# Regrouping the second layer norms of a two-layer attention and expert kernel: seven batches beside layer 0's last steps, with their norms on GpSimd

## The chip, the cores and the metric

The kernel runs on one core of a Trainium2 chip. Times are microseconds of device time. The engines are named as in the profile: PE (TensorE matmul), DVE (VectorE), ACT (ScalarE), POOL (GpSimd) and SP (SyncE, which only issues transfers here). [...]The core has an on-chip memory, from which all engines work, and eight accumulation banks, into which PE writes.

## What is computed

The input is 8 batches of 512 tokens with 256 features. Two layers follow each other, each of the form x + attention(norm(x)) + feed-forward(norm(x)):

```python
xn = _layernorm(x, axis=-1)
x = x + _L0_attn_ref(xn, ...) + _L0_ffn_ref(xn, ...)   # 16 heads; 8 experts, one for each token
xn = _layernorm(x, axis=-1)
x = x + _L1_attn_ref(xn, ...) + _L1_ffn_ref(xn, ...)   # two causal attentions with a convolution between; low-rank gelu
return x
```

In layer 0's feed-forward every token goes to the one expert whose centroid it is most like; the expert (norm, 256 to 1024, relu, 1024 to 256) gives ye, and the result is alpha * ye + (1 - alpha) * x with alpha a sigmoid. In layer 1's feed-forward, a product of rank 64 leads up to 1024 features, a gelu follows, and a product of rank 64 leads back to 256. The norm between the layers, the second norm, needs layer 0's whole sum for a token: input, attention and expert. It is this norm, with what leads to it, that the change moves.

## The kernel before

The running sum of each batch stays in an on-chip tile `acc[b]` (128 tokens x 4 chunks x 256). The kernel has three stages.

**Layer 0.** Attention runs as 32 jobs (8 batches x 4 groups of 4 heads). The function `run` (L420) goes through steps t = 0 to 268; a job takes 8 steps for its scores (the matmul at L323, then on DVE the row maximum at L340), and 12 steps later 8 steps for its exps (the matmul at L372, the exponential on ACT at L399); between lie four products with the values (L412). When a job is complete, `l0_done` (L840) transposes and divides its output on DVE (L843 to L847) and POOL adds it to `acc` (L851). Scores are only made in steps 0 to 255; in the last 13 steps exps and value products remain. After the matmuls of each step, `Work.fill` (L103) lets other work in. It first takes work with a due time close by (projections, values, the shift of the maxima, which also issues four transfers on SP's queue, L360), and otherwise draws on a generator, `stream` (L782). Each `yield` of a number charges the generator that much; it may draw while the room of the step, which grows by `MOE_PER_STEP` each step, is above zero. A `yield At(n)` makes the generator wait for step n. So the generator's order is that of program text, and the steps give it its pace.

The generator first makes the first norms and the routing, then the 23 expert blocks of 256 tokens. A block gathers its weights with a POOL-issued transfer (L708) and ends with `output` (L763), whose result goes to a DRAM tile `fs_d` in sorted order (L778). When all 23 are done, `second_norm` (L453) follows for the first four batches (`N_LATE = 4`).

`second_norm` does this for a list of batches. It gathers a batch's rows from `fs_d` with four indirect transfers issued by POOL (L462, into one of two `fg` buffers), one batch ahead. Three steps later DVE adds alpha times the rows to `acc` (L477) and takes mean and variance (`Norms.stats`, L219 and L220). After the last batch `Norms.close` (L222) makes reciprocal deviations: DVE, one square root on ACT (L227), DVE. Then for each batch, one step apart, ACT norms four chunks into a tile `yn` (L236), POOL adds the layer 1 biases to `acc` (L486), and one step later PE transposes the normed tile into features (`to_features`, L241; the copies out of the bank are DVE's for one half, L247, and ACT's for the other, L249). Layer 0's attention tail has a single bank for these transposes.

**Layer 1's feed-forward** (L911 to L978). Eight batches, each in four pairs: `ffn_in` (L912) once a batch, `ffn_hidden` (L923; matmul L927, two gelus on ACT, L933) one pair ahead, `ffn_rank` (L938, matmul L940), and `ffn_out` (L945) at a batch's end: a DVE copy (L947), matmuls (L952), and DVE sums into `acc` (L956). The second norms of batches 4 to 7 run here, as the generator `late`, one piece a pair.

```python
        late = second_norm(range(NB - N_LATE, NB), "d", lambda n: n)
        next(late)
        pTs = {0: ffn_in(0)}
```

**Layer 1's attention** with its convolution follows, from L980, and is not touched.

Of the kernel before, what the change touches and what calls it, by code (L numbers as in the profile page):

```python
# [9 lines left out]
F32 = mybir.dt.float32  # L10
# [3 lines left out]
ALU = mybir.AluOpType  # L14
# [5 lines left out]
P = 128  # L20
NB = 8
S = 512
D = 256
NC = S // P
# [12 lines left out]

STEPS = (8, 6)
LEAD = (12, 12)
N_LATE = 4  # L40
MOE_PER_STEP = 2.05
LAG = 7


# [93 lines left out]
def block_kernel(ctx: ExitStack, tc: tile.TileContext, x, a0_wqk, a0_bqk, a0_wv, a0_bv, cent, experts,  # L138
                 a1_wqk, a1_bqk, a1_wv, a1_bv, conv_w, conv_b, out_w, out_b, u1, v1, f_b1, u2, v2, f_b2, out):
    nc = tc.nc  # L140
# [5 lines left out]
    big = ctx.enter_context(tc.tile_pool(name="big", bufs=NB))  # L146
# [5 lines left out]
    acc = []  # L152
# [49 lines left out]
    class Norms:  # L202
# [27 lines left out]
                nc.vector.tensor_scalar(self.rs1, rs[:, 0, :], 1.0, None, ALU.add)  # L230
            nc.vector.scalar_tensor_tensor(self.nm_t, self.mv[:, :, 0], -1.0, rs[:, 0, :], ALU.mult, ALU.mult)

        def norm(self, i, dst):
            for c in range(NC):
                n = i * NC + c
                nc.scalar.activation(  # L236
                    dst[:, c, :], acc[self.bs[i]][:, c, :], AF.Identity, bias=self.nm_t[:, n : n + 1],
                    scale=self.rs[:, 0, n : n + 1],
                )
# [210 lines left out]
            attend(t)  # L450
        work_of.drain()

    def second_norm(bs, nm, pause):  # L453

        norms = Norms(mid, bs, nm, False)
        fgs = {}

        def gather(b):
            fgs[b] = mid.tile([P, NC, D], F32, tag="fg", name=f"fg{b}", bufs=2)
            for c in range(NC):  # L460
                t = b * NC + c
                nc.gpsimd.indirect_dma_start(  # L462
                    out=fgs[b][:, c, :],
                    out_offset=None,
                    in_=fs_d[:, :],
                    in_offset=IndirectOffsetOnAxis(ap=pos_i[:, t : t + 1], axis=0),
                )

        gather(bs[0])
        for i, b in enumerate(bs):  # L470
            if i + 1 < len(bs):
                gather(bs[i + 1])
            yield pause(3)
            for c in range(NC):
                t = b * NC + c
                a = acc[b][:, c, :]
                nc.vector.scalar_tensor_tensor(a, fgs[b][:, c, :], alpha[:, t : t + 1], a, ALU.mult, ALU.add)  # L477
            norms.stats(i)
        norms.close()
        yns = {}  # L480
        for i in range(len(bs) + 1):
            if i < len(bs):
                b = bs[i]
                yns[b] = work.tile([P, NC, D], F32, tag="o", name=f"yn{b}")
                norms.norm(i, yns[b])
                nc.gpsimd.tensor_tensor(acc[b], acc[b], ob_sb.unsqueeze(1).to_broadcast([P, NC, D]), ALU.add)  # L486
            if i > 0:
                b = bs[i - 1]
                t = big.tile([P, 2, S], F32, tag="xT", name=f"yT{b}")
                for k in range(2):  # L490
                    to_features(yns[b], t, 0, k, f"c{b}")
                xT1.append(t)
            yield pause(1)

    xT = []
    pos_i = const.tile([P, NT], I32, name="pos_i")
# [26 lines left out]
    with ExitStack() as l0:  # L523
# [258 lines left out]
        def stream():  # L782

            norms = [first_norms] + [Norms(pre, bs, nm, True) for bs, nm in (((1, 2, 3), "b"), ((4, 5, 6, 7), "e"))]
            of = {b: (n, i) for n in norms for i, b in enumerate(n.bs)}
            xns = {}

            def stats(b):
                of[b][0].stats(of[b][1])

            def norm(b):
                xns[b] = first_norm(*of[b])

            def features(b):
                first_features(b, xns.pop(b))

            def close(i):
                norms[i].close()

            do = {"s": stats, "c": close, "n": norm, "f": features, "a": affinities}  # L800
            for t, pieces in enumerate(FIRST):
                for p in pieces.split():
                    do[p[0]](int(p[1]))
                if t == 1:
                    for n in range(NBLK):
# [12 lines left out]
            yield At(todo.t + 5)  # L818
            banks_experts()
            nxt.features()  # L820
            yield 0.5
            for n in range(NBLK):
                blk = nxt
                for f2 in range(NFC // 2):
                    blk.hidden(f2)
                    yield 1.75
                    if f2 == 0 and n + 1 < NBLK:
                        nxt = Block(moe, n + 1)
                if n + 1 < NBLK:
                    nxt.features()  # L830
                    yield 0.5
                for j in range(TB // P):
                    blk.output(j)
                    yield 3.5
            banks_alone()
            yield from second_norm(range(NB - N_LATE), "c", lambda n: At(todo.t + n))

        todo = Work()

# [71 lines left out]
    with tc.tile_pool(name="ffn", bufs=1, side="right", reuse_waits="tile") as ffn:  # L911
        def ffn_in(b):  # L912
            ps = bank()
            for k in range(2):
                nc.tensor.matmul(
                    ps, lhsT=u1_sb[:, k, :, :].rearrange("p i r -> p (i r)"), rhs=xT1[b][:, k, :],
                    start=(k == 0), stop=(k == 1),
                )
            pT = ffn.tile([P, S], F32, tag="pT", name=f"pT{b}", bufs=2)
            nc.vector.tensor_copy(pT, ps)  # L920
            return pT

        def ffn_hidden(b, c2, pT):  # L923
            ps = [bank("hidden") for _ in range(2)]
            for i in range(2):
                fc, r = 2 * c2 + i, slice(i * RANK, (i + 1) * RANK)
                nc.tensor.matmul(  # L927
                    ps[i], lhsT=v1_sb[r, fc * P : (fc + 1) * P], rhs=pT[r, :], start=True, stop=True
                )
            hT = ffn.tile([P, 2, S], F32, tag="hT", name=f"gT{b}_{c2}", bufs=3)  # L930
            for i in range(2):
                fc = 2 * c2 + i
                nc.scalar.activation(  # L933
                    hT[:, i, :], ps[i], AF.Gelu_apprx_tanh, bias=fb1_sb[:, fc : fc + 1]
                )
            return hT

        def ffn_rank(pq, c2, hT):  # L938
            for i in range(2):
                nc.tensor.matmul(  # L940
                    pq[i * RANK : (i + 1) * RANK, :], lhsT=u2_sb[:, 2 * c2 + i, :], rhs=hT[:, i, :],
                    start=(c2 == 0), stop=(c2 == NFC // 2 - 1),
                )

        def ffn_out(b, pq):  # L945
            qT = ffn.tile([P, S], F32, tag="qT", name=f"fqT{b}", bufs=2)
            nc.vector.tensor_copy(qT, pq)  # L947
            for h in range(2):
                ps = bank()
                for j in range(2):  # L950
                    c = 2 * h + j
                    nc.tensor.matmul(  # L952
                        ps[:, j * D : (j + 1) * D], lhsT=qT[:, c * P : (c + 1) * P], rhs=v2_sb, start=True, stop=True
                    )
                a = acc[b][:, 2 * h : 2 * h + 2, :].rearrange("p c d -> p (c d)")
                nc.vector.tensor_tensor(a, a, ps, ALU.add)  # L956

        share_banks(hidden=banks[:4], mm=banks[4:7])
        late = second_norm(range(NB - N_LATE, NB), "d", lambda n: n)
        next(late)  # L960
        pTs = {0: ffn_in(0)}
        ahead = [(0, 0, ffn_hidden(0, 0, pTs[0]))]
        pairs = [(b, c2) for b in range(NB) for c2 in range(NFC // 2)]
        pq = None
        out_of = None
        for n, (b, c2) in enumerate(pairs):
            next(late, None)
            if c2 == 1 and b + 1 < NB:
                pTs[b + 1] = ffn_in(b + 1)
            if n + 1 < len(pairs):  # L970
                nb, nc2 = pairs[n + 1]
                ahead.append((nb, nc2, ffn_hidden(nb, nc2, pTs[nb])))
            _, _, hT = ahead.pop(0)
            if c2 == 0:
                pq = banks[7]
            ffn_rank(pq, c2, hT)
            if c2 == NFC // 2 - 1:
                ffn_out(b, pq)  # L978
# [238 lines left out]
```

## Time and profile before

| | us |
|---|---|
| median of 3 runs | 2176.61 (2166.74 to 2185.63) |
| the profiled execution | 2178.01 |
| its span in the profile | 2176.2 |
| PE busy | 2069.3 (95%) |
| DVE busy | 1235.2 (57%) |
| ACT busy | 862.9 (40%) |
| POOL busy | 195.5 (9%) |

All stretches below are in microseconds from the start of that span. Layer 0 runs to 1052, the feed-forward from there to about 1176, layer 1's attention after it. A group of instructions is named by its line, engine and tiles. A PE record's end is modelled, so a busy PE need not be a PE at its peak; each f32 matmul of the program appears as two records. The granted clock is the share of full TensorE speed. In the chain of waits, each piece is followed back to what released it; "issue" is time in which an engine waited for nothing that the profile shows.

### The profile page before, as it was taken

The numbers are of one execution on the slowest core, as the hardware profiler recorded it, in microseconds if no ns is written. First come the engines' busy times: TensorE is split into PE (matmuls) and PEld (weight loads), VectorE is DVE, ScalarE is ACT, GpSimd is POOL, SyncE is SP. The second block draws the span as 40 slices with busy tenths as digits, with TensorE's granted clock in tenths as the row PEclk, the third lists the DMA queues.
The fourth block names the chain that finished last, engine by engine and source line by source line (L and its number), as shares of the span: only waits on it lengthen the run. The fifth ranks groups of instructions, "written<-read, shape, count | busy, mean of one in ns | idle before, by whom it ended". The sixth has DMA issues, their size and how long they took to land.

```text
span 2176.2 us, 35488 instructions
## 1 busy us (share of the span) xinstructions
PE 2069.3 (95%) x13664; PEld 1049.0 (48%) x13664; DVE 1235.2 (57%) x3569; ACT 862.9 (40%) x1674; POOL 195.5 (9%) x222
## 2 busy tenths in 40 slices
PE   7997999999999999997698999999999999999998
PEld 4532555555555555552233455555545545554553
DVE  5465454555555555555423666666766666666661
ACT  2343333333333333334442344444444444444442
POOL 4355000000000000004410000000000000000000
PEclk7599999999999999997899899999999999999997
DMA  5013212221221222201100000000000000000000
GB/s 205 1 42 111 93 61 98 97 100 54 103 94 60 91 73 93 102 11 56 58 1 0 2 2 2 2 2 12 2 12 2 12 2 12 2 12 2 12 2 20
DMA packets 37064, 93.53 MB, mean 43 GB/s; under 512 B 5792, under 2 KB 27936, under 8 KB 33952
## 3 DMA queue, kind: packets, MB, share of 16 engines
q0 software_dynamic: 6384, 59.78, 7.5%
q1 hardware_dynamic: 29792, 30.56, 4.3%
q8 instruction: 107, 1.75, 0.3%
q10 hardware_dynamic: 720, 0.93, 0.1%
q14 instruction: 61, 0.50, 0.1%
HBM read 70.03 MB, written 20.45 MB: 42 GB/s over the span
## 4 chain that ended last, share of the span: by engine, by line
PE 80%; DVE 5%; issue 3%; ACT 1%; another core or an unknown queue 0%; POOL 0%; DMA 0%; DVEq 0%; POOLq 0%; ACTq 0%
PE bank L323 26%; PE bank L412 12%; PE bank L746 8%; PE bank L767 8%; PE bank L272 4%; PE bank L1023 4%; PE bank L390 4%; PE bank L372 3%; PE bank L282 2%; PE bank L1041 2%; PE bank L927 1%; PE bank L1075 1%; PE bank L940 1%; DVE jk L343 1%; PE bank L245 1%
## 5 line engine op out<-in xcount | busy, mean ns | idle before, releaser
L399 ACT ACTIVATE e<-bank 128x512 f32<-128x512 f32 (+1 forms) x1280 | 640.2, 552 | 964.6 <-PE bank L372 483.7
L323 PE MATMUL bank<-k,q 32*128 32x512 f32 (+3 forms) x3072 | 778.9, 538 | 24.4 <-DVE m L340 21.0
L372 PE MATMUL bank<-q,k 32*128 32x512 f32 (+3 forms) x3072 | 701.6, 536 | 15.4 <-DMA q<-mT 13.5
L343 DVE CUSTOM_DVE_ANT_0 jk<-bank,cmask 128x512 bf16<-128x512 f32 (+3 forms) x1024 | 502.6, 491 | 238.0 <-PE bank L323 159.3
L323 PEld LDWEIGHTS bank<-k,q 32*128 32x128 f32 x3072 | 304.3, 187 | 390.4 <-issue 165.2
L340 DVE TENSOR_REDUCE m<-bank 128x1 f32<-128x512 f32 x512 | 329.2, 685 | 163.5 <-PE bank L372 121.0
L412 PE MATMUL bank<-e,v 128*32 128x512 f32 (+3 forms) x3072 | 321.7, 506 | 0.7 <-ACT e L399 0.7
L372 PEld LDWEIGHTS bank<-q,k 32*128 32x128 f32 x3072 | 271.2, 187 | 37.1 <-issue 26.9
L746 PE MATMUL bank<-hsT,w 128*128 128x256 f32 x736 | 180.8, 391 | 0.7 <-ACT e L399 0.7
L767 PE MATMUL bank<-w,hT 128*128 128x256 f32 x736 | 169.0, 383 | 0.0
L746 PEld LDWEIGHTS bank<-hsT,w 128*128 128x128 f32 x736 | 134.5, 191 | 70.4 <-issue 53.3
L767 PEld LDWEIGHTS bank<-w,hT 128*128 128x128 f32 x736 | 136.1, 190 | 35.6 <-issue 19.0
L412 PEld LDWEIGHTS bank<-e,v 128*32 128x32 f32 x3072 | 67.9, 109 | 143.1 <-issue 136.9
L390 PE MATMUL bank<-mask_t,ident_bf 128*128 128x128 bf16 (+1 forms) x768 | 124.3, 244 | 0.0
L390 PEld LDWEIGHTS <-ident_bf 128*128 128x128 bf16 x768 | 43.7, 97 | 158.4 <-issue 143.2
L759 DVE TENSOR_SCALAR hT<-bank,w 128x256 f32<-128x256 f32 x92 | 44.5, 484 | 113.4 <-ACT hT L757 113.4
L1023 PE MATMUL bank<-ctxT,cw_sb 128*128 128x256 f32 x384 | 90.0, 383 | 2.1 <-DVE q L262 1.8
L343 DVE DVE_READ_ACCUMULATOR2_ANT m<- 128x1 f32 x1024 | 84.9, 83 | 0.4
L264 ACT ACTIVATE k<-bank,bqk,rows 128x512 f32<-128x512 f32 x64 | 46.2, 773 | 81.5 <-PE bank L272 71.5
L851 POOL TENSOR_TENSOR acc<-acc,og 128x256 f32<-128x256 f32 x32 | 23.2, 726 | 615.2 <-DVE og L847 615.2
L776 DVE TENSOR_TENSOR f<-bank,w 128x256 f32<-128x256 f32 x46 | 19.5, 425 | 101.4 <-PE bank L767 101.4
L1023 PEld LDWEIGHTS bank<-ctxT,cw_sb 128*128 128x128 f32 x384 | 70.1, 189 | 13.2 <-DVE q L262 3.2
(180 smaller groups left out, 1472.4 us busy)
## 6 DMA issues: line engine op xcount, KB each, us to landing
q<-mT SPq DMA_DIRECT2D x384, 2.0 KB
hs_d<-zeros SPq DMA_DIRECT2D x23, 256.0 KB
hs<-hs_d SPq DMA_DIRECT2D x23, 256.0 KB
fs_d<-f SPq DMA_DIRECT2D x23, 256.0 KB
acc<-in_x SPq DMA_DIRECT2D x8, 512.0 KB
out<-acc SPq DMA_DIRECT2D x8, 512.0 KB
cw_sb<-in_conv_w SPq DMA_DIRECT2D x1, 768.0 KB
wqk<-in_a_wqk ACTq DMA_DIRECT2D x1, 512.0 KB
```

What stands on the lines that cost most here:

```text
L264: nc.scalar.activation(dst, ps, AF.Identity, bias=bias[:, half : half + 1], scale=rows[:, half : half + 1])
L272: nc.tensor.matmul(ps, lhsT=w[:, k, col : col + P], rhs=src[:, k, :], start=(k == 0), stop=(k == 1))
L323: lambda h=h, qc=qc, at=at, nk=nk: nc.tensor.matmul(heads[h % 2][:, at : at + nk], lhsT=self.q[h * PH : (h + 1) * PH, qc * P : (qc + 1) * ...
L340: nc.vector.tensor_reduce(self.m[:, qc, h, :], src, AX.X, ALU.max, negate=True)
L343: nc.vector.tensor_tensor_reduce(out=junk[:, :nk], in0=src, in1=cmask[:, S - nk :], scale=1.0, scalar=-3e38, op0=ALU.add, op1=ALU.max, acc ...
L372: lambda h=h, kc=kc, at=at, lo=lo: nc.tensor.matmul(heads[h % 2][:, at : at + S - lo], lhsT=self.k[h * PH : (h + 1) * PH, kc * P : (kc + 1 ...
L390: nc.tensor.matmul(heads[h][:, : len(blocks) * P], lhsT=ident_bf, rhs=mask_t[:, : len(blocks) * P], start=False, stop=True,)
L399: nc.scalar.activation(e[:, h, :], heads[h][:, :n], AF.Exp, scale=self.scale)
L412: nc.tensor.matmul(self.av[h * PH : (h + 1) * PH, lo:], lhsT=self.v[:, kc, 4 * self.g + h, :], rhs=es[h // 2][:, h % 2, :], start=first, s ...
L746: nc.tensor.matmul(ps[:, i * TB : (i + 1) * TB], lhsT=w[:, O_W1 + k * FF + fc * P : O_W1 + k * FF + (fc + 1) * P], rhs=self.hsT[:, k, :], ...
L767: nc.tensor.matmul(ps[:, 0:D], lhsT=self.hT[:, fc, j * P : (j + 1) * P], rhs=w[:, O_W2 + fc * D : O_W2 + (fc + 1) * D], start=(fc == 0), s ...
L1023: nc.tensor.matmul(ps[:, :w], lhsT=cw_sb[:, k, tap, c * P : (c + 1) * P], rhs=ctxT[b % 2][:, k, tap + lo : tap + lo + w], start=(k == 0 an ...
```

## The change

The second norms are no longer two lists of four batches but three groups, of which the first two, with seven batches, run as part of layer 0's generator. The third, batch 7 alone, has its gather and its expert sum there, and the rest in the feed-forward's first pairs. Between the gather of one batch and its sum lie two steps in place of three. The four norms of a batch are POOL `tensor_scalar` instructions (multiply, then add, with two scalars for each partition) in place of ACT's. The experts' allowance a step goes from 2.05 to 2.1.

```diff
-N_LATE = 4
-MOE_PER_STEP = 2.05
+SECOND = ((0, 1, 2, 3), (4, 5, 6), (7,))
+MOE_PER_STEP = 2.1
...
-        def norm(self, i, dst):
+        def norm(self, i, dst, eng=None):
             for c in range(NC):
                 n = i * NC + c
+                if eng is not None:
+                    eng.tensor_scalar(
+                        dst[:, c, :], acc[self.bs[i]][:, c, :], self.rs[:, 0, n : n + 1], self.nm_t[:, n : n + 1],
+                        ALU.mult, ALU.add,
+                    )
+                    continue
...
+    def second_norm(norms, i):
+
+        b = norms.bs[i]
+        yn = work.tile([P, NC, D], F32, tag="o", name=f"yn{b}")
+        norms.norm(i, yn, nc.gpsimd)
+        nc.gpsimd.tensor_tensor(acc[b], acc[b], ob_sb.unsqueeze(1).to_broadcast([P, NC, D]), ALU.add)
+        return yn
...
+    def second_norms():
+
+        gather(0)
+        for g, bs in enumerate(SECOND):
+            norms = Norms(mid, bs, "cde"[g], False)
+            seconds_of.append(norms)
+            for i, b in enumerate(bs):
+                if b + 1 < NB:
+                    gather(b + 1)
+                yield At(todo.t + 2)
+                add_experts(b)
+                if g < 2:
+                    norms.stats(i)
+            if g == 2:
+                return
+            yield At(todo.t + 1)
+            norms.close()
+            yns = {}
+            for i in range(len(bs) + 1):
+                if i < len(bs):
+                    yns[i] = second_norm(norms, i)
+                if i > 0:
+                    second_features(bs[i - 1], yns.pop(i - 1))
+                yield At(todo.t + 1)
...
             banks_alone()
-            yield from second_norm(range(NB - N_LATE), "c", lambda n: At(todo.t + n))
+            yield from second_norms()
...
-        late = second_norm(range(NB - N_LATE, NB), "d", lambda n: n)
-        next(late)
+        def late():
+            norms = seconds_of[-1]
+            yield
+            norms.stats(0)
+            yield
+            norms.close()
+            yield
+            yn = second_norm(norms, 0)
+            yield
+            second_features(norms.bs[0], yn)
+
+        rest = late()
...
-            next(late, None)
+            next(rest, None)
```

The functions `gather`, `add_experts` and `second_features` hold what stood inside `second_norm` before: the four gathers of a batch, its four DVE sums, and its transposes.

More of the change, by code (lines that the diff above doesn't have):

```diff
@@ L451, in run @@
         work_of.drain()
[L453 to L493, printed above, removed]
@@ new lines, in block_kernel, with gather, add_experts @@
+    fgs = {}
+    seconds_of = []
+    def gather(b):
+        fgs[b] = mid.tile([P, NC, D], F32, tag="fg", name=f"fg{b}", bufs=2)
+        for c in range(NC):
+            t = b * NC + c
+            nc.gpsimd.indirect_dma_start(
+                out=fgs[b][:, c, :],
+                out_offset=None,
+                in_=fs_d[:, :],
+                in_offset=IndirectOffsetOnAxis(ap=pos_i[:, t : t + 1], axis=0),
+            )
+    def add_experts(b):
+        for c in range(NC):
+            t = b * NC + c
+            a = acc[b][:, c, :]
+            nc.vector.scalar_tensor_tensor(a, fgs[b][:, c, :], alpha[:, t : t + 1], a, ALU.mult, ALU.add)
@@ new lines, in second_norm, with second_features @@
+    def second_norm(norms, i):
[4 more added lines that the diff above has]
+        return yn
+    def second_features(b, yn):
+        t = big.tile([P, 2, S], F32, tag="xT", name=f"yT{b}")
+        for k in range(2):
+            to_features(yn, t, 0, k, f"c{b}")
+        xT1.append(t)
+    def second_norms():
[21 more added lines that the diff above has]
+                yield At(todo.t + 1)
```

## The prediction

> **What bounds the kernel now.** I read the 40 slices first, then a table of stretches cut at the stage borders, then the chain of waits and the order of time inside the bad stretches. The slices (54.4 us each) show TensorE full except at the start and around slices 18 to 21:
>
> ```profile
> PE   7997999999999999997698999999999999999998
> ```
>
> The table of stretches (columns: stretch, its length, busy us of PE, weight loads, DVE, ACT, POOL with instruction counts, granted clock, DMA share, GB/s):
>
> ```profile
> 900.00:966.00 66.00, 64.81 (x364) 33.80 (x357) 35.05 (x64) 24.76 (x46) 2.41 (x3) 1.00 0.13 47
> 976.00:1008.00 32.00, 23.61 (x109) 6.75 (x105) 20.17 (x47) 9.46 (x18) 16.21 (x17) 0.76 0.26 75
> 1008.00:1052.00 44.00, 34.60 (x153) 11.09 (x145) 13.38 (x37) 28.21 (x51) 10.13 (x5) 0.82 0.09 27
> 1052.00:1081.00 29.00, 15.70 (x48) 4.33 (x45) 18.85 (x57) 7.46 (x13) 16.28 (x17) 0.77 0.33 101
> 1112.00:1173.00 61.00, 57.07 (x209) 19.56 (x210) 13.01 (x19) 24.00 (x39) 0.00 (x0) 1.00 0.00 0
> ```
>
> Up to 976 (the last expert matmul ends at 975.6) PE is the bound at full clock. 976 to 1052 is layer 0's tail: attention steps 246 to 268 without expert work, with the first four second norms. 1052 to 1173 is the feed-forward stage; its first 29 us hold the other four. In the three stretches from 976 to 1081 PE has gaps and a clock near 0.8. The reader is to see that the change can win only between 976 and 1100, about 6% of the span.
>
> In the feed-forward stage the PE-bound rhythm is read from the chain of waits: the copies of a batch's rank-64 result start at
>
> ```profile
> 1098.91 0.70 DVE fqT L947
> ...
> 1111.91 0.70 DVE fqT L947
> ...
> 1124.91 0.70 DVE fqT L947
> ```
>
> 13.0 us per batch. The first such copy starts only at 1080.15, 28.1 us after the stage's first matmul (1052.0), and the second 18.8 us later. In the order of time, ACT sits from 1066.0 to 1079.5 at the square root of the late norms, behind four batches of gathers, sums and statistics on DVE; the gelus behind it wait, and PE waits for them.
>
> In the tail, this chain piece stands out, with PE, DVE and ACT all standing:
>
> ```profile
> 989.54 6.97 another core or an unknown queue
> ```
>
> It ends just after the gather traffic does (last packets before 996). No view names its cause.
>
> **What the Trainium skill says.** TensorE: Matmul & The Clock Gate, What's actually happening: PE's clock halves after an idle window and comes back after a busy one. The trace agrees: clock 0.50 from 990 to 998, where an AV group takes 1.94 us instead of 1.06. So a PE gap costs more than its length. ScalarE: Activation LUTs, What ACT_TABLE_LOAD costs: some 1283 ns for each change of set; the trace has 1.28 us at each of the loads at 1017.0, 1022.6, 1064.8, 1082.4. GPSIMD Engine Reference, Engine selection: one-input elementwise work is roughly line-rate there, two-input work about twice slower than on VectorE. The trace agrees for one form and not for another, which is my main unknown:
>
> ```profile
> L565 POOL TENSOR_SCALAR acc<-acc,rs1e,nme x16: 552/553/555, 161.3 to 207.3; 128x256 f32<-128x256 f32 x16
> ...
> L553 POOL TENSOR_SCALAR h<-acc,mve,rse x16: 1222/1228/1237, 55.7 to 73.8; 128x256 f32<-128x256 f32 x16
> ...
> L486 POOL TENSOR_TENSOR acc<-acc,ob_sb x8: 2348/2354/2368, 1022.7 to 1095.0; 128x1024 f32<-128x1024 f32 x8
> ...
> L236 ACT ACTIVATE yn<-acc,nmc,rsc x16: 584/594/608, 1020.5 to 1036.8; 128x256 f32<-128x256 f32 x16
> ```
>
> (from the answers by line and by tile: count, then min/median/max ns). The new norm on POOL multiplies and adds with two per-partition scalars, as L565 does (553 ns), but writes another tile, as L553 does (1228 ns, subtract then multiply). I take 0.553, as the operation pair is the same; 1.23 is the upper end, and below 0.553 nothing in the trace gives a reason to go.
>
> **The change part by part.** Following the planner's rule (room per step, costs, due times), before: last expert output in step 245, gathers from 246, sums in 249, 252, 255, 258, norms 258 to 261. After: last expert output in step 240, end seen in 242, sums of batches 0 to 3 in 244, 246, 248, 250, close and norms 251 to 254, features to 255, gather 5 in 256, sums 4 to 6 in 258, 260, 262, close and norms 263 to 265, features to 266; batch 7's sum falls in the final drain, after step 268.
>
> *More expert work per step.* Nothing in sum while PE is full: 64.81 of 66 us busy. Attention of steps 241 to 245 moves behind the experts: 5 x 1.29 (scores and exps matmuls) + 2 x 1.05 (AV) + 0.2 = 8.8 us, so experts end at 966.8. The expert weight loads on POOL's queue come 2.4% closer together, hidden: POOL is busy 5 us in 100 there. Bounds from other stalls: PE idles about 8 us between 300 and 900, so some 3 us either way.
>
> *Steps 241 to 243*: 2.07 us each, as steps 246 to 250 take now: 973.0.
>
> *Steps 244 to 250*: DVE is the bound. Per batch four sums at 0.41 spacing (1.65) and four statistics pairs at 0.53 and the rest (2.3), 3.95 us; per step two max reductions, 1.29; one output transpose group 1.4; one shift copy 0.3. So 4 x 3.95 + 7 x 1.29 + 1.7 = 26.5; plus 1 us because the first sum, two steps rather than three after its gather, meets rows that land about 9.5 us after the last expert result (979.13, the first gather now, is 3.5 after it; four at 1.25; landing 1): 1000.5. DVE's sums stand ahead of the reductions that free score banks, so PE waits behind them.
>
> *Steps 251 to 255*: reductions 1.3 and close 1.2, to 1003. Then POOL in order: norm 4 x 0.553 = 2.21, bias add 2.35, and PE's transposes (in program order between attention steps) wait for each norm. Four norms with three bias adds between: 8.8 + 7.1 = 15.9, to 1019. ACT did this norm in 2.07 beside POOL's add; now both are serial, 4.6 per batch. Last features 2, and 3 for cold-clock matmuls (transposes 1.12 instead of 0.66 per four): 1024. Removed: 16 ACT norms, 8.3 us, that stood between the exps.
>
> *Steps 256 to 262*: 7 x 1.93 (1041 to 1051 has 3.85 for two such steps), to 1037.5; sums, statistics, gathers 5 to 7 (5 us each on POOL) run beside it. The third of these gathers ends near 1040, and close near 1041.
>
> *Steps 263 to 268*: three norms, two adds: 6.6 + 4.7 = 11.3, features 2, two steps 3.9: 1058.5. Now 1052.0, so the tail ends **6.5 us later**. The extra table pair of the second close (2.6 us) lies on an ACT that only has two exps a step, 1.09; no queue waits for more than that, so I give it the same cover as the waits above.
>
> *SP's queue* gets no new transfer in the tail; a shift transfer of 4 parts in step 249 and one in 257 now meet more gather traffic, with three steps until the exps need them: nothing, or 3 us if they land late.
>
> *Feed-forward stage.* First rank matmul 4.7 us after the start (1056.7 - 1052.0), 7 batches at 13.0, last batch's four pairs 10.3: 106.0. Added: batch 7's sum ahead of the first copy on DVE 1.65, its 8 transposes 1.1, two table loads 2.6 of which ACT's slack (gelus take 1.27 of each 3.05 us pair) hides about 1.1, 1.5 left. 110.3 against 121.2 (1052.0 to 1173.2). The stall goes; the next late thing is PE itself. **10.9 us won**; with a last copy counted from 1174.4 it is 12.3; I use 12. If batch 7's close blocks the gelus as the late norms do now, 5 of it go.
>
> Sum: +6.5 - 12 = -5.5. The profiled execution took 2178.0 (span 2176.2, 1.8 around it), 1.4 above the median 2176.6. So 2172.5 on its scale, **2171** on the median's.
>
> **Rivals.** *Room in the tail* (faster). The 7 us stall is an accident that does not come back, and POOL's norms overlap better than the sum allows, ACT being free. Then the tail is what PE needs: 1045 now without the stall, less ACT's queue at 1020 to 1040 (5), plus three batches of features (6.6), less the idle before the close (4): 1042.6, so -9.4 - 12 = -21: 2155. For it: ACT is busy 14.87 of the 20 us from 1020. Against: DVE's 26.5 us is arithmetic on the same instructions.
>
> *POOL as the bound* (slower). Norms at L553's 1.23: 28 x 0.675 = 19 more on the norm chain: tail at 1077, +25 - 12 = +13: 2190; with a repeat of the 7 us stall under 28 gathers, 2197. It decides from about 0.75 us a norm (5.5 / 28 above 0.553). For it: L553, and DVE's sums with two SBUF inputs run beside it. Against: L565's operations.
>
> *It does not do what it says*: norms slip past step 268 into the drain. The planner's dates exclude it for all but batch 7; 2 in 100, at about the time of before.
>
> **From cases to numbers.** Forecast 58, room 25, POOL 15, nothing done 2. For 1% (21.8 us, about what a measurement of this kernel can tell from no change): below 2155 lies half of the room case and a little of the forecast's spread, 0.19; above 2198 a third of POOL's, 0.05; the rest 0.76. The range takes the forecast's unknowns (3 expert phase, 5 cold clock, 3 shift, 5 close; about 12 together), most of the room case and half of POOL's: 2151 to 2190.
>
> **What would show it.** Last expert matmul near 967; norms on POOL at 0.55; first feed-forward matmul near 1058; first rank copy under 22 us after it; 13.0 between the rest. Wrong if the feed-forward start comes before 1046 or after 1068, or POOL's norm is over 0.75.

## The result and the profile after

| | before | after |
|---|---|---|
| median, same chip | 2176.07 (8 runs) | 2194.68 (8 runs; 2191.65 to 2205.81) |
| ratio | | 1.0093 (95% interval 1.0068 to 1.0118) |
| the profiled execution | 2178.01 | 2192.13 |
| its span | 2176.2 | 2190.4 |

The change makes the kernel 0.9% slower: 14.2 us between the two profiled spans, where 5.5 were to be won. All stretches below are microseconds from the start of the span of the kernel named.

The 40 slices of the kernel after, its rows for PE and for the granted clock (tenths):

```profile
PE   7997999999999999997898999999999999999998
...
PEclk7599999999999999998799799999999999999997
```

By the slices PE is as full as before. What differs must be looked for in the stretches. The table of stretches of the kernel after (stretch, length, busy us of PE, weight loads, DVE, ACT, POOL, granted clock, DMA share, GB/s):

```profile
900.00:966.00 66.00, 64.82 (x350) 34.67 (x349) 34.30 (x62) 23.68 (x44) 2.41 (x3) 0.97 0.13 47
976.00:1012.00 36.00, 28.24 (x143) 7.75 (x141) 29.78 (x74) 13.08 (x23) 20.18 (x21) 0.86 0.28 81
1012.00:1052.00 40.00, 29.20 (x147) 9.77 (x147) 24.59 (x63) 18.71 (x34) 31.02 (x34) 0.91 0.20 63
1052.00:1074.00 22.00, 17.54 (x57) 6.50 (x60) 2.36 (x5) 7.68 (x13) 13.48 (x15) 0.55 0.01 5
...
1112.00:1173.00 61.00, 56.91 (x206) 18.65 (x205) 12.40 (x18) 24.08 (x39) 0.00 (x0) 1.00 0.00 1
```

976 to 1074 is the tail. From 976 to 1012 DVE is the busiest engine (29.78 of 36 us: sums, statistics, row maxima); from 1012 to 1052 POOL is (31.02 of 40 us: norms, bias additions, gathers); from 1052 on PE is (17.54 of 22 us), at a clock of 0.55.

The chain of waits of the kernel after shows the feed-forward's rank copies:

```profile
1093.02 0.70 DVE fqT L971
...
1106.90 0.70 DVE fqT L971
...
1119.90 0.70 DVE fqT L971
```

The first starts 18.4 us after the stage's first matmul (1074.6), where 28.1 were needed before; the second 13.9 us after it, not 18.8; then 13.0 each, as before. This part of the change works. The tile view of the norms on POOL (count, min/median/max ns):

```profile
L237 POOL TENSOR_SCALAR yn<-acc,rsc,nmc x16: 549/556/559, 1014.2 to 1030.6; 128x256 f32<-128x256 f32 x16
L237 POOL TENSOR_SCALAR yn<-acc,rsd,nmd x12: 544/552/556, 1052.5 to 1063.2; 128x256 f32<-128x256 f32 x12
```

So the time is lost ahead of that stage and behind it. Four marks divide the span: the last expert matmul's end, the feed-forward's first matmul, the start of its last rank copy, and the first division of layer 1's attention (L1044 in the kernel before).

| stretch | before | after | difference | predicted |
|---|---|---|---|---|
| experts, to their last matmul | 975.7 | 976.5 | +0.8 | -8.8 |
| tail, to the first feed-forward matmul | 76.3 | 98.1 | +21.8 | +15.3 |
| feed-forward, to its last rank copy | 122.4 | 107.8 | -14.6 | -12 |
| layer 1's lead-in, to its first division | 60.7 | 67.3 | +6.6 | 0 |
| the rest of layer 1 | 941.1 | 940.7 | -0.4 | 0 |

The predicted +15.3 of the tail is 6.5 + 8.8: the prediction counted the tail's end, and its start was to come 8.8 earlier. Two terms failed outright, the experts and the lead-in; the tail was over 40% dearer. Both columns are single executions: the tail before, 76.3 us here, was 67.3 and 81.2 us in two other profiles of the same instructions, so the tail's difference lies between 17 and 31 us.

### The profile page after: what moved, and what is told of

The parts are those of the page before. It is cut to its first block, busy times and chain, and to the rows that moved or that the text cites. A ratio compares the mean times of both kernels' runs of the same rounds, so it can differ in the third digit from the quotient of the medians.

```text
span 2190.4 us, 35505 instructions
## 1 busy us (share of the span) xinstructions
PE 2080.9 (95%) x13664; PEld 1053.3 (48%) x13664; DVE 1236.7 (56%) x3572; ACT 850.5 (39%) x1645; POOL 212.5 (10%) x254
## 4 chain that ended last, share of the span: by engine, by line
PE 82%; DVE 5%; issue 2%; ACT 1%; POOL 0%; DMA 0%; SPq 0%; DVEq 0%; ACTq 0%; POOLq 0%
PE bank L329 26%; PE bank L418 12%; PE bank L770 8%; PE bank L791 8%; PE bank L278 5%; PE bank L396 4%; PE bank L1057 4%; PE bank L378 3%; PE bank L288 2%; PE bank L1075 2%; PE bank L951 2%; PE bank L964 1%; PE bank L1109 1%; PE bank L251 1%; DVE m L346 1%
## 5 line engine op out<-in xcount | busy, mean ns | idle before, releaser
L405 ACT ACTIVATE e<-bank 128x512 f32<-128x512 f32 (+1 forms) x1280 | 640.1, 552 | 978.8 <-PE bank L378 507.8
L378 PE MATMUL bank<-q,k 32*128 32x512 f32 (+3 forms) x3072 | 705.6, 539 | 15.7 <-DMA q<-mT 13.8
L800 DVE TENSOR_TENSOR f<-bank,w 128x256 f32<-128x256 f32 x46 | 19.5, 424 | 108.9 <-PE bank L791 108.9
```

The source lines that it names most:

```text
L378: lambda h=h, kc=kc, at=at, lo=lo: nc.tensor.matmul(heads[h % 2][:, at : at + S - lo], lhsT=self.k[h * PH : (h + 1) * PH, kc * P : (kc + 1 ...
L405: nc.scalar.activation(e[:, h, :], heads[h][:, :n], AF.Exp, scale=self.scale)
```

## The experiments

All ratios are to the kernel before on the same chip. The letters in the expectations: theory A, that the higher allowance brings no earlier end of the experts; rival C, that the serial chain of norms and bias additions on POOL sets the tail; theory D came after the first four runs and is told with the ones that follow. PE's busy time in one fixed stretch of the expert phase, 230 to 966, carried most of it. The other columns are the stretches above, in us ("rest" is the rest of layer 1):

| kernel | PE busy, 230 to 966 | last expert matmul | tail | feed-forward | lead-in | rest | ratio |
|---|---|---|---|---|---|---|---|
| before | 726.1 | 975.7 | 76.3 | 122.4 | 60.7 | 941.1 | |
| before_leadin | 726.1 | 973.6 | 67.3 | 122.1 | 59.6 | 943.7 | 1.0016 |
| paced_late | 726.1 | 976.6 | 81.2 | 118.8 | 61.0 | 941.1 | 0.9996 |
| gathers_apart | 726.2 | 977.1 | 85.2 | 124.8 | 65.5 | 933.3 | 1.0002 |
| allow21_alone | 720.8 | 974.2 | 95.3 | 122.1 | 64.7 | 945.8 | 1.0146 |
| allow206 | 720.4 | 982.5 | 94.6 | 123.1 | 60.6 | 946.7 | 1.0087 |
| odd_filled | 733.5 | 964.4 | 74.0 | 124.0 | 63.8 | 941.1 | 0.9952 |
| odd_leadin | 733.5 | 967.7 | 75.1 | 122.5 | 59.6 | 945.4 | 0.9971 |
| after | 720.8 | 976.5 | 98.1 | 107.8 | 67.3 | 940.7 | 1.0093 |
| warm_leadin | 720.8 | 978.8 | 98.1 | 107.8 | 59.4 | 943.2 | 1.0042 |
| warm_tail | 720.8 | 976.4 | 98.1 | 107.8 | 67.3 | 940.7 | 1.0100 |
| norms_on_act | 720.7 | 976.1 | 118.0 | 106.8 | 65.6 | 946.7 | 1.0117 |
| bias_last | 720.7 | 978.6 | 109.7 | 106.8 | 60.7 | 941.0 | 1.0088 |
| regroup_205 | 726.2 | 977.0 | 102.4 | 108.3 | 64.7 | 933.5 | 1.0030 |
| change_odd_filled | 732.7 | 954.5 | 111.0 | 106.8 | 67.2 | 946.6 | 0.9992 |
| change_odd_leadin | 733.0 | 952.0 | 100.7 | 107.7 | 59.4 | 943.3 | 0.9982 |
| change_odd_warm | 734.1 | 955.7 | 117.5 | 107.9 | 59.4 | 944.9 | 0.9975 |

The ratios are over many executions; the stretches are of one each, and they differ between executions of the same instructions. Up to the feed-forward, before, before_leadin and paced_late are the same program, with tails of 76.3, 67.3 and 81.2 us; so are change_odd_filled and change_odd_leadin, with 111.0 and 100.7. The end of the experts differs by up to 3.7 us in this way, and the rest of layer 1, the same instructions in all, takes 933.3 to 946.7 us. A smaller difference than these between two rows says nothing by itself. PE's busy time in the expert phase agrees within 1.4 us.

### The allowance alone

```diff
-MOE_PER_STEP = 2.05
+MOE_PER_STEP = 2.1     # in the kernel before
```

> The kernel before with the experts' allowance at 2.1 and nothing else. Theory A (the higher allowance itself loses what the earlier end should have won): last expert matmul at 974 to 978 although it now belongs to step 240, so the five attention steps behind it come on top; feed-forward starts near 1061 instead of 1052, time 2184 to 2188. Rival B (the allowance costs nothing, all of the loss lies in the regrouped norms): last expert matmul near 967, feed-forward start 1050 to 1054, time within 4 us of before.

Measured: 1.0146 (1.0115 to 1.0176). The last expert matmul ends at 974.2, 1.5 us earlier instead of 8.8, which is within the spread of the kernel before, and the tail behind it grows to 95.3 us. The part of the change that was to shorten the expert phase makes the kernel slower by itself. In the profile most of that lies in the tail, 19.0 us longer where five attention steps make 8.8.

### Norms on ACT again, and bias additions behind the norms

```diff
-        norms.norm(i, yn, nc.gpsimd)     # norms_on_act, in the kernel after
+        norms.norm(i, yn)
```

> The changed kernel with its second norms back on ACT, all else kept. Theory A (the norms' engine is not the cause, PE comes late anyway because of the clock and of DVE): feed-forward starts within 4 us of 1074.6, time 2190 to 2199. Rival C (the POOL chain of norm and bias add, 4.6 us a batch, sets the pace): ACT's 2.1 us a batch lets the feed-forward start 8 us or more earlier, time 2187 or less.

Measured: 1.0117 (1.0086 to 1.0148); the feed-forward starts at 1094.1, 19.5 us later than with the change. Neither expectation came. Two pieces of 6.4 and 7.8 us without a named cause stand in this tail (more on such pieces below), and the interval overlaps that of the change (1.0068 to 1.0118), so this shows no gain from ACT's norms, but not that POOL's are better.

```diff
-        nc.gpsimd.tensor_tensor(acc[b], acc[b], ob_sb...)   # bias_last: out of second_norm,
+            for b in bs:                                    # and behind all norms of a group
+                add_biases(b)
```

> The changed kernel with POOL's bias adds after the last norm of each group instead of between the norms. Theory A: PE waits mostly for DVE and for its own clock, so the feed-forward starts at most 4 us earlier than 1074.6, time 2190 to 2195. Rival C (serial POOL chain): five bias adds of 2.35 us leave the chain, feed-forward starts about 11 us earlier, time 2183.

Measured: 1.0088 (1.0056 to 1.0121), the change's own ratio within its interval, with the feed-forward starting at 1088.3, later. Two pieces without a named cause make 10.0 of the 13.7 us, and the experts end 2.1 later. Rival C is not borne out: its 2183 us would be a ratio of 1.003, below the interval. In this run the stretch from 1060 to 1088 has a clock of 0.55.

### The late norms paced, nothing moved into the tail

The kernel before, where batches 4 to 7 stay in the feed-forward but in two groups (4, 5) and (6, 7), with gathers, sums, norms (on POOL) and transposes spread over 15 pairs by hand.

```diff
-        late = second_norm(range(NB - N_LATE, NB), "d", lambda n: n)
-        next(late)
+        LATE = ("g4", "", "g5", "s4", "g6", "s5", "cd", "n4 g7", "n5 f4 s6", "f5", "s7", "ce", "n6", "n7 f6", "f7")
+        late = paced()     # g gathers, s sums, c closes, n norms, f makes features
```

> The kernel before with its four late batches kept in the feed-forward stage but spread over 15 pairs in two groups of two: a gather every second pair, the sum three pairs after its gather, square root and norm a pair apart, norms on POOL. If the stall of the stage was only one of order (waits queued ahead of the gelus and of the rank copies), the tail stays as before (start at 1052), the first rank copy comes 17 to 20 us after the start, the last near 1162, time 2162 to 2167. If transfers or table loads hold the stage up anyway, time 2174 or more.

Measured: 0.9996 (0.9972 to 1.002). The first copy comes 19.1 us after the stage's start, but the next ones at 16.0, 19.4 and 14.8 us, not 13.0: the one stall of 28 us became several small ones (6.4 of the 19.1 us are again a piece without a named cause). The expected gain did not come; the ratio answers to the rival's 2174 us or more.

### Why a higher allowance loses PE time

The order of time on PE in the kernel after, near the end of the experts (start, us, line, tiles; in brackets the idle time before and what ended it; lines 329 and 378 are the matmuls of scores and exps, 418 the value products, 791 an expert's):

```profile
968.26 1.06 PE L418 MATMUL bank<-e,v 128*32 128x512 f32 x8
969.25 0.70 PE L329 MATMUL bank<-k,q 32*128 32x512 f32 x2
969.27 0.70 PE L378 MATMUL bank<-q,k 32*128 32x512 f32 x2
969.79 0.59 PE L329 MATMUL bank<-k,q 32*128 32x512 f32 x2
969.80 0.59 PE L378 MATMUL bank<-q,k 32*128 32x512 f32 x2
971.16 1.29 PE L329 MATMUL bank<-k,q 32*128 32x512 f32 x3 [0.76 <-DVE m L346]
```

The step that starts at 969.25 got no expert work: its scores are followed at once by those of the next step, at 971.16, and these wait 0.76 us for DVE's row maxima to free a bank. While experts run only two banks hold scores (`banks_experts`), one step's worth. A step that has a value product or expert work covers the maxima; value products come only in even steps. This is theory D: in an **empty odd step** PE waits up to 1.2 us (9.9 us in 12 waits in the kernel before, 0.8 on average), and it is the allowance's size against the pieces' charges that decides how many such steps there are. The planner's rule gives 11 at 2.05, 21 at 2.06 and 19 at 2.1, up to the experts' end. The waits of PE from 230 to 966 (us in total, times, longest), before:

```profile
PE bank L323 <- DVE m L340: 9.9, 12, 1.2
```

and after:

```profile
PE bank L329 <- DVE m L346: 15.2, 18, 1.2
```

The 5.3 us more are the 5.3 us that PE's busy time falls in that stretch. This reading agrees with the Trainium skill, Perfetto Trace Analysis, Optimization Strategy: the same gap repeating on the engine that should be saturated can mean too few buffers for the next tile. No run gave the scores a third bank, which would test that directly; the runs below change only how many steps go empty.

An allowance hardly above the old one, and two kernels with a rule that lets no odd step go empty (a charge is taken in advance if need be), test it:

```diff
-            if not forced and (n == most or self.room <= 0):
+            if not forced and (n == most or (self.room <= 0 and (n > 0 or t % 2 == 0))):
                 return
...
                     self.room -= cost
+                    n += 1
```

> The kernel before with the allowance at 2.06 in place of 2.05. By the planner's rule the last expert output moves by one step only (244 for 245), but the steps that hold neither expert or projection work nor a value product rise from 11 to 21. Theory D (in such a step PE waits about 1 us for the row maxima, as only two banks hold scores): last expert matmul at 983 to 986, PE's waits for the maxima between 230 and 966 rise from 9.9 to 15 us or more, time 8 to 14 us above before. Rival E (what costs is the pace itself, or the longer tail after the experts): 0.01 of allowance changes nothing, last expert matmul at 974 to 976, time within 3 us of before.

> The kernel before at 2.05 with one rule more in the planner: in a step without a value product (odd steps) one piece of work is drawn even when the allowance is used up. Last expert output stays in step 245; steps with nothing in them fall from 11 to 5. Theory D: last expert matmul 5 to 7 us earlier, at 969 to 971, time 2170 to 2172 on the first chip's scale, 5 to 7 us below before. Rival E: within 2 us of before.

> The changed kernel with the same rule: last expert output in step 239 instead of 240, steps with nothing in them fall from 19 to 4. Theory D: last expert matmul at 960 to 963 instead of 976.5, feed-forward start at 1058 to 1063 instead of 1074.6, time about 14 us below the changed kernel, so within 6 us of before. Rival E: as the changed kernel, 0.9% above before.

Measured: with 2.06 the ratio is 1.0087 (1.0057 to 1.0117), the waits 15.6 us in 22 times, the last expert matmul at 982.5: half a per cent of allowance costs 0.9% of time. With the rule in the kernel before the ratio is 0.9952 (0.9927 to 0.9977), the last expert matmul at 964.4 and the waits

```profile
PE bank L324 <- DVE m L341: 2.3, 4, 0.6
```

With the rule in the changed kernel: 0.9992 (0.9977 to 1.0007), the last expert matmul at 954.5, 22 us earlier than with the change, and the waits at 1.7 us in 3 times. So theory D holds for the expert phase: in each of the three runs PE's waits and the end of the experts move as it says. With the rule the experts end 11.3 and 22.0 us earlier, of which 7.6 and 13.5 are waits for row maxima that are gone; the rule also draws work ahead of its allowance, and the rest was not told apart.

The theory does not cover the tail. Of what allow206 loses in its profile, 6.8 us lie in the expert phase and 18.3 in the tail, whose mean clock is 0.66 where the kernel before has 0.80; why is not known. With the rule in the changed kernel 13 of the 22 us go to a tail of 111.0 us, but 4.5 of these are a piece without a named cause, and change_odd_leadin, the same program up to there, has 100.7.

### The 7 us stall

In the kernel before a stall of 6.97 us at 989.5 had no named cause. It ended with the gathers' traffic; if gathers that overlap cause it, gathers held back take it away. The edit, shown without the flag that keeps it to the tail's four batches:

```diff
-            if i + 1 < len(bs):
-                gather(bs[i + 1])
             yield pause(3)
...
                 nc.vector.scalar_tensor_tensor(a, fgs[b][:, c, :], alpha[:, t : t + 1], a, ALU.mult, ALU.add)
+            if i + 1 < len(bs):
+                gather(bs[i + 1])
             norms.stats(i)
```

> The kernel before with the tail's gathers issued one batch at a time, each after the sum of the batch ahead of it, so that no two batches of row transfers follow each other without a gap. Theory F (the 7 us in which PE, DVE and ACT stand is set off by eight row gathers in a row): no such piece in the chain of waits between 976 and 1050, tail 69 to 73 us instead of 76 to 81, time 4 to 8 us below before. Rival G (it comes from something else, or the later gathers only move the wait to DVE's sums): a piece of 4 us or more is still there, or the sums wait that long, time within 3 us of before or above.

Measured: 1.0002 (0.9986 to 1.0018). No such piece is in this tail's chain of waits, but the tail is 85.2 us, with a clock of 0.50 from 1030 to 1060. Inconclusive. Such pieces of 2 to 8 us are in the tails of 8 of the 17 profiles here, before among them, and not in that of the kernel after. They do not go with the program: before_leadin has none and ends its tail after 67.3 us, with the same instructions up to there. All four profiles from one chip have them, none of the seven from two others. Their cause stays open.

### The regrouping alone, and the cold clock

```diff
-MOE_PER_STEP = 2.1      # regroup_205, in the kernel after
+MOE_PER_STEP = 2.05
...
+            if layer == 0 and t >= 259:     # warm_tail; in warm_leadin: layer == 1 and t < lead, banks[6]
+                nc.tensor.matmul(banks[0], lhsT=ident, rhs=xT1[0][:, 0, :], start=True, stop=True)
             work_of.fill(t, per_step, most)
```

The added matmul writes a bank that is free there, and nobody reads it.

> The change with the allowance back at 2.05: regrouping and POOL norms alone. Theory D (the higher allowance makes steps in which PE waits for row maxima, and gives no earlier end) expects the last expert result at 975.7 as before (976.5 with the change), and puts a price of about 15 us on the higher allowance in the kernel before; but here it also moved the second group's norms in front of step 268, and at 2.05 the norms of batches 5 and 6 fall behind step 268 with nothing beside them. So a tail of 100 to 110 us (98.1 with the change), the feed-forward at 107 to 108, time 2185 to 2200. The rival, that the allowance is the whole loss and the regrouping is worth its -5.5 us: tail under 90, time 2165 to 2175.

> The change with one more f32 matmul, 128x128 by 512 columns, in each of steps 259 to 268 of layer 0, whose result nobody reads: ten times about 0.9 us of PE work at full clock, mostly where PE waits now (8.9 us idle between 1050 and 1080). If the halved clock is what makes the tail's last part long (from 1052.5 to 1074.6, 22.1 us, clock 0.50 to 0.57), the clock stays over 0.8 there and the stretch from the fourth norm's start to the feed-forward takes 17 to 20 us, time 3 to 6 us under the change's. If the chain of norms on POOL sets it and the clock is only its companion, the stretch stays at 22 or grows to 30 and the time is the change's or up to 9 us more.

> The change with one more such matmul in each of the first 12 steps of layer 1, into a bank that is free then. From the last rank copy to the first token division the change takes 67.3 us with the clock at 0.50 to 0.75 between 1200 and 1240, before 60.7. Twelve matmuls are 10 us of PE work at full clock. If the light steps let the clock fall (PE waits for row maxima there), the clock is near 1.00 and the lead-in takes 58 to 64 us in spite of the added work: time 2185 to 2192. If the clock falls for another reason, the lead-in is 75 to 80 us and the time 2202 to 2208.

> The change with the rule for odd steps and both sets of added matmuls. With that rule alone the tail was 111 us (954.5 to 1065.5), the lead-in 67.2, time 2183. If the cold clock is the reason that the 22 us won in the expert phase were given back, the tail is 98 to 103, the lead-in 58 to 64, time 2165 to 2172, under the kernel before and about the best so far (2174.6). If not, 2190 to 2203.

Measured for **regroup_205**: 1.0030 (1.0009 to 1.0051), tail 102.4. PE's busy time in the expert phase is back at 726.2 and the waits at 9.9 us. So at 2.05 the regrouping loses 0.3%, and the allowance 0.6% on top (1.0093 against 1.0030). In the other order the allowance loses 1.5%, and the regrouping then wins 0.5% (1.0093 against 1.0146). The two parts do not simply add up: by the planner's rule, at 2.05 the norms of batches 5 and 6 fall behind step 268, with nothing beside them. Neither pair was run on one chip.

For **warm_tail**: 1.0100 (1.0066 to 1.0134), no gain. The clock from 1052 to 1074 rose from 0.55 to

```profile
1052.00:1074.00 22.00, 18.16 (x76) 6.51 (x74) 2.47 (x5) 10.98 (x17) 13.51 (x15) 0.92 0.06 15
```

and the stretch from norm 4's start (1055.0) to the feed-forward's start (1074.5) took 19.4 us, in place of 22.1. But the four added matmuls in it are 4.2 us of PE work, and those ahead of it made norm 4 start 2.5 us later. By this count, an estimate (19.4 less 4.2), the halved clock lengthens the tail's last part from some 15 us to 22; extra work does not buy it back.

For **warm_leadin**: 1.0042 (1.0023 to 1.0062), half a per cent under the change. The lead-in of the kernel after, from 17.7 to 63.7 us behind the last rank copy:

```profile
1200.00:1246.00 46.00, 43.97 (x193) 20.36 (x192) 24.86 (x94) 10.01 (x19) 0.00 (x0) 0.67 0.00 1
```

and with the added matmuls:

```profile
1202.00:1248.00 46.00, 45.70 (x267) 19.74 (x265) 30.14 (x111) 13.82 (x26) 0.00 (x0) 1.00 0.01 1
```

PE is busy in both, but after the change a record lasts longer: the clock is 0.67, and 193 matmul records fit where 267 do with the clock at 1.00 (24 of them the added ones). Twelve more matmuls, an estimated 12 us of work by their 1.05 us in warm_tail, make the lead-in 8 us shorter.

For **change_odd_warm**, with the rule for odd steps and both sets: 0.9975 (0.9952 to 0.9997), a median of 2172.2 us. The lead-in is 59.4 us as expected; the tail is 117.5 us, not 98 to 103, so that half of the expectation missed, as warm_tail did. The profiled execution, at 2187.1 us, is the second slowest of 21, and says little of where the median's gain lies.

### Does the cold lead-in belong to the change?

The added matmuls of warm_leadin in three other kernels: the kernel before, odd_filled and change_odd_filled.

> The kernel before with the twelve added matmuls in layer 1's first steps. If the cold lead-in belongs to the change, the lead-in here goes from 60.7 to 60 or more (its clock is lifted only from 0.66 to 0.86 up, and 10 us of work are added): ratio 0.999 to 1.003. If it is a habit of every arrangement, in the mean over runs the clock in the lead-in is as low here as there, and the time falls by 0.3 to 0.5% (the changed kernel went from 1.0093 to 1.0042): ratio 0.995 to 0.997.

> The kernel before with the rule for odd steps and the added matmuls. Alone the rule gave 0.9952. If the two add up: 0.990 to 0.993, 2159 to 2165 us beside 2180. If the lead-in gains nothing in this arrangement: 0.995 to 0.998.

> The change with the rule for odd steps and the added matmuls in layer 1 only. With the rule alone 0.9992, with both sets of added matmuls 0.9975. If the regrouping by itself is worth its -5.5 us when expert phase and lead-in are equal, this is 0.2 to 0.3% under odd_leadin: 0.988 to 0.990. If its longer tail takes back what the feed-forward wins, it is 0.2 to 0.5% above odd_leadin: 0.994 to 0.997.

Measured: before_leadin 1.0016 (1.0000 to 1.0033), nothing gained: its lead-in is 59.6 us, before it was 60.7. odd_leadin 0.9971 (0.9954 to 0.9988), change_odd_leadin 0.9982 (0.9968 to 0.9996). By the rule set down for before_leadin, the cold lead-in would belong to the change. The profiles do not bear that out. With the added matmuls the lead-in is 59.4 to 59.6 us in every kernel. Without them it is 67.2 to 67.3 us in after, warm_tail and change_odd_filled, but 60.7 in bias_last, which has the change too; and gathers_apart, which has not, takes 65.5 us with a clock of 0.67. Nor is the gain of 0.5% found again: with the rule for odd steps, the added matmuls move the changed kernel from 0.9992 to 0.9982, with intervals that overlap. In the stretch of the kernel before that answers to the one shown, the clock is

```profile
1192.00:1238.00 46.00, 44.26 (x225) 19.91 (x222) 29.53 (x110) 12.89 (x24) 0.00 (x0) 0.81 0.01 1
```

The instructions there are the same in both kernels. So a low clock makes the lead-in long, which warm_leadin shows; what lets it fall in one kernel and not in another stays open.

With the rule and the warm lead-in in both, the change is worth nothing that can be told: 0.9982 against 0.9971, with intervals that overlap, medians of 2167.2 and 2169.6. In the profiles its experts end 15.7 us earlier and its feed-forward is 14.8 us shorter, and 25.6 of these 30.5 us go into a tail of 100.7 us in place of 75.1. The lowest ratio is that of odd_filled, the kernel before with one rule changed, at 0.9952; odd_leadin, which adds the matmuls, is no better.

## Why the prediction was wrong, point by point

**The step that failed** is the first of the sum, "More expert work per step. Nothing in sum while PE is full". It moved 8.8 us of attention behind the experts and let them end at 966.8. They ended at 976.5. The count of 64.81 busy us in 66 was right for the kernel before, but it is no property of PE: it was what that allowance left. PE waits, 0.8 us on average, in the empty odd steps, and the new allowance made eight more of them. 5.3 us of the 9.7 missing are seen as lost busy time from 230 to 966, 0.8 at 971; the other 3.6 have no account, where the prediction left 3 open either way. That the empty steps are the cause is shown by the rule that fills them: with it the changed kernel's experts end at 954.5, and its ratio falls from 1.0093 to 0.9992. In the ratios the allowance costs 0.6% with the regrouping and 1.5% without it, where the step counted nothing in sum. The other two terms, +6.5 and -12, make -5.5 us, or -0.25%, for the regrouping; it measured +0.3% at 2.05, where its norms fall behind step 268, and -0.5% at 2.1.

**Layer 1's lead-in** had no term: +6.6 in the profile, and warm_leadin shows that the clock makes it. Since bias_last, with the change, has none of it, a term for the change would not have been right either. The prediction's range had 5 us for the cold clock in the tail only.

**The tail's steps**, measured from the experts' end, follow the prediction until the last: sums and statistics end at +35.5 (+33.7 predicted), the four norms with features at +58.0 (+57.2), steps 256 to 262 take 13.6 (13.5), norm 4 starts at +76.0. Then 22.1 us where "11.3, features 2, two steps 3.9" make 17.2. The term was mis-sized by the clock. The order of time on PE after shows it:

```profile
1053.10 2.08 PE L251 MATMUL bank<-ident,yn 128*128 128x128 f32 x4 [2.09 <-POOL yn L237]
1055.96 1.11 PE L251 MATMUL bank<-ident,yn 128*128 128x128 f32 x4 [0.79 <-DVE yT L253]
1057.01 1.94 PE L418 MATMUL bank<-e,v 128*32 128x512 f32 x8
1058.88 2.08 PE L378 MATMUL bank<-q,k 32*128 32x512 f32 x4
```

Each group takes nearly twice its time at full clock (1.11 for 0.66, 1.94 for 1.06). PE waited for the first norm of the second group, and behind that wait the clock is low; with the clock at 0.92 in warm_tail, the same part took 19.4 us with 4.2 us of added matmuls in it. The prediction's own remark that a PE gap costs more than its length was applied to 3 us of transposes, and not to the attention steps behind them.

**Right**: in the tail DVE is the busiest engine during the sums and POOL during the norms; a POOL norm takes 0.55 us, so the rival of POOL as the bound is wrong, although its 2190 lies close to what came; the 7 us stall did not return, which is luck, since such pieces come and go between executions of one program; SP's queue cost 0.2 us at most where PE waits for a shift (1041.7); the feed-forward won 14.6 where 12 were counted: batch 7's work there is hardly seen, as the second copy follows after 13.9 us and the others after 13.0. Two small slips of the working changed nothing: 122.4 less 110.3 is 12.1, not 12.3, and the value product of 1.94 us starts at 999.46, behind the stretch named for it.

**The rival of room in the tail** fell too: a lighter ACT did not shorten the tail, in which DVE (29.78 of 36 us) and then POOL (31.02 of 40 us) are busy. That POOL's chain sets the pace there is read from these shares; bias_last, which shortens the chain, did not end the tail earlier.

Of the 19.7 us between -5.5 and +14.2, 9.6 are the expert phase, 6.5 the tail and 6.6 the lead-in, less 2.6 from the feed-forward and 0.4 from the rest.

## What to carry to other kernels

A stage in which the bounding engine is 98% busy is full under one order of work; before a pace is changed, count in the new order the steps that leave a double buffer uncovered, for each of them may cost a wait. Work moved out of a stage where it stalls must be charged at its new place with that place's own bound, and with the clock there: behind a gap in the tail here, matmuls took nearly twice as long. A knob that looks like a rate may act through rounding: 2.05, 2.06 and 2.1 gave 11, 21 and 19 empty steps. And one profile is one execution: before a stretch of it is given a cause, look at a second profile of the same instructions.

## What the runs showed of the hardware that was not expected

- The clock fell to 0.50 in stretches where PE has hardly a gap: from 1226 to 1242 in the kernel after, 16 us with PE busy throughout, mostly on matmuls of 32 rows. One 128x128 by 512 matmul in each step kept it at 1.00. Thin matmuls alone do not bring it down: in the kernel before, matmuls of the same lines ran at 1.00 from 1220 to 1234, with PE busy for 13.98 of 14 us. The Trainium skill, TensorE: Matmul & The Clock Gate, A second HAM failure mode: psum-queue depth-cycling, tells of a clock that swings because PE idles briefly between groups; before that stretch there are four waits of 0.2 to 0.4 us and one of 0.5, from 1204 to 1223, which fits, but no run here tests it.
- The time of a run follows its mean clock: the runs of one kernel, allow21_alone, give 2204 us at 0.949, 2215 at 0.944 and 2224 at 0.937.
- A POOL instruction with two scalars for each partition takes 0.55 us for 128x256 numbers when it multiplies and adds (L237), and 1.22 us when it subtracts and multiplies (L553 before).
